# A state space layer on Trainium2: half of a product of the powers' last doubling made on ScalarE, table steps and the last group's work in another order

## The chip, the core and the metric

The kernel runs on one core of a Trainium2 chip (trn2). The metric is the device time of one execution in microseconds (us), the median of several. A core has five engines that run side by side, each with an instruction queue of its own worked through in order: TensorE (PE in the profile; its weight loads are PEld), VectorE (DVE), ScalarE (ACT), GpSimd (POOL) and SyncE (SP), which here only issues DMAs. They wait for each other through semaphores.

## The reference

The kernel computes one block over x (4096 rows of 512) with a context of 3202 rows of 384. The cross-attention layer keeps the 32 highest scores per row and head, and gives scale and shift ("film") for what goes into and out of a diagonal state space layer. Feed-forward layers follow. The change lies in the state space layer and at its two borders. Cut to that:

```python
def s4d(x, log_dt, A_re, A_im, C_re, C_im, D_skip):
    dt = jnp.exp(log_dt)
    A = A_re + 1j * A_im
    C = C_re + 1j * C_im
    dtA = dt[:, None] * A                     # 512 channels x 64 states
    dC = C * (jnp.exp(dtA) - 1.0) / A
    powers = jnp.exp(dtA[:, :, None] * jnp.arange(L))
    K = 2.0 * jnp.einsum('dn,dnl->dl', dC, powers).real
    ...                                       # y = causal convolution of x with K
    return y + x * D_skip

x = layernorm(x_text) * (1 + gate * scale_in) + gate * shift_in
y = s4d(x, ...) * (1 + gate * scale_out) + gate * shift_out
xt = x_text + y
xt = xt + gelu(layernorm(xt) @ W1 + b1) @ W2 + b2
```

## The kernel before

**Attention.** `attention` works through 128 slots (32 row tiles of 4 heads) and 8 more that drain the pipeline. A slot k does `threshold(k)` on VectorE, the logarithm of the softmax sum of head k-1 (`log_sum`, L624), its Exp (`softmax`, L648), and parts of older tiles on TensorE: `transposed` (L664), `weighted` (L685), `film` (L710), `reverse` (L752), the last of which stores the layer's input to DRAM (`x1r`, L757). A DMA on POOL adds the heads of a tile up in SBUF (L659). Engines keep the order in which the code issues (`manual_schedule`).

**Tables.** `state_space_tables` (L886) is a generator. It computes on VectorE, with a few Tanh and Sin on ScalarE, the powers of exp(dtA) that the layer needs and stores them to a DRAM scratch `tabs` (`store`, L900: powers of two on SP's queue, the rest on POOL's). `TABLE_SLOTS` (L348) says after which slots it is resumed: after 128 (loads, first exponential up to the Tanh L943), twice after 129 (angles; Tanh and Sin, L958 to L962), after 130 (six squarings) and after 134 (chunk powers and output coefficients).

**State space layer.** Channels lie in pairs: 256 pairs in 8 groups of 32. A group's work is spread over rounds g = -2 to 8 of `round_` (L1323). For a group:

- `powers(g, k)`, k = 0 or 1 (L1117): powers 0 to 63 of 16 pairs by doubling on VectorE, real and imaginary parts; five levels of two products (L1132, L1133) and a sum (L1134), into one of five power tiles of 16 KB a partition.
- `top(g, k)` (L1136): the last doubling, powers 64 to 127. ScalarE makes the product with the real factor, an activation per pair (L1140, 16 of 128x128). VectorE makes the product with the imaginary factor, two halves of 8 pairs (L1150, two of 128x1024). `top_sum` (L1153) adds them later, half by half (L1156).
- `turn` and `chunk` (L1160, L1175), u = 0 to 7: TensorE transposes four pairs' powers (L1170), ScalarE evicts them to `bt` (L1173), TensorE multiplies them with x (L1182), ScalarE evicts to the states `ht` (L1186).
- `scan_inside`, `scan_over`, `scan_into` (L1212 to L1227): recurrences over chunks on VectorE, from all of `ht`.
- `outputs` (L1229): VectorE weighs the states into `z` (L1237 to L1239), ScalarE copies z to `sz` (L1244).
- `between(g, u)`, u = 0 to 3 (L1250): TensorE products of sz and powers (L1257), in two PSUM buffers; ScalarE evicts to `yg` (L1263), POOL adds the skip term (L1265), and four DMAs on SP store rows to the scratch `kd` (L1267).
- `load_k` (L1272) reads kd back as shifted rows `hk` (two DMAs of 512 KB, four buffers), `inside` (L1283) multiplies them with x (L1291), `store` (L1296) evicts (L1298) and stores to `yT` (L1300).

In round g VectorE does scan_inside(g), top_sum(g+1, 1), scan_over(g), scan_into(g), outputs(g), powers(g+2, 0), its part of top(g+2, 0), powers(g+2, 1), top_sum(g+2, 0), and its part of top(g+2, 1). In the same round TensorE and ScalarE do turn and chunk of group g+1 with inside and store of group g-1 between them, then between(g, 0 and 1), turn and chunk 7, between(g, 2 and 3). Short-lived VectorE tiles (`tmp`, among them z and the products of top) share five buffers.

**Feed-forward.** `feed_forwards` (L1419) starts on its own weights pool, which lies where the power tiles lay. `weights(0)` (L1933) loads the first quarter of the weights on POOL's queue; `load_front(i)` (L1475) loads, for a row tile, yt from yT, x and the film rows on SP's queue. `front_a` to `front_d` (L1498 to L1528) make the layer's normalized and transposed input, and `hidden` (L1536) begins.

Of the kernel before, what the change touches and what calls it, by code (L numbers as in the profile page):

```python
# [20 lines left out]
P = 128  # L21
# [325 lines left out]
HALVES = ((0, 401), (401, 400))  # L347
TABLE_SLOTS = [NT * H + k for k in (0, 1, 1, 2, 6)]  # L348


def attention(env, io, x1r, film_out, missed, masked, tabs):
# [11 lines left out]
    with ExitStack() as ctx:  # L363
# [149 lines left out]
        setup2 = ExitStack()  # L513
        at_pool = []

        xts, xns, qT, m8s, s_of, nms, lbs, aTs, pts, pas, acTs, x1s, fs = (
# [242 lines left out]
        def slot(i, h):  # L759
# [5 lines left out]
            back = 0 <= j < NT  # L765
            log_sum(k - 1)
            if k < NT * H:
                threshold(k)
# [79 lines left out]
        for k in range((NT + 2) * H):  # L848
            if k == H:
                setup2.close()  # L850
                at_pool.append(
                    ctx.enter_context(tc.tile_pool(name="f_at", bufs=1, reuse_waits="tile"))
                )
            slot(*divmod(k, H))
            if k == NT * H:

                flat = [s_pool[0].tile([P, GP4], F32, name="s") for _ in range(2)]
                flat.append(kT.rearrange("p h g -> p (h g)"))
                steps = state_space_tables(nc, io, tabs, [
                    f[:, 3 * k * NPAIR : 3 * (k + 1) * NPAIR].rearrange("p (k q) -> p k q", k=3)  # L860
                    for f in flat for k in range(4)
                ])
            for _ in range(TABLE_SLOTS.count(k)):
                next(steps, None)
            if k < H:
                for v in range(NDV):
                    part(k, v)
# [18 lines left out]
def state_space_tables(nc, io, tabs, planes):  # L886
# [9 lines left out]
    for name in ("log_dt", "A_re", "A_im", "C_re", "C_im"):  # L896
        v[name] = new()
        nc.sync.dma_start(v[name], io[name])

    def store(k, t):  # L900
# [40 lines left out]
    k, r = exp_before(v["log_dt"])  # L941
    t = new()
    nc.scalar.activation(t, r, AF.Tanh, scale=0.5)  # L943
    yield
    dt = v["log_dt"]
# [63 lines left out]
    ts(w3[:, 2, :], w3[:, 1, :], -1.0, None, ALU.mult)  # L1009
    store(T_CHUNK + 6, w3)  # L1010

    er, den, ei = rc, kc, w[:, 1, :]
# [41 lines left out]
def state_space(env, io, tabs, x1r, yT):  # L1054
# [9 lines left out]
    with ExitStack() as ctx:  # L1064
# [71 lines left out]
        def top(g, k):  # L1136
# [8 lines left out]
            for half in range(2):  # L1145
# [3 lines left out]
                t2 = temp(NSB * n).rearrange("p (q r n) -> p q r n", q=NSB // 2, r=2)  # L1149
                mul(t2, pt[:, js, :, :n], wi.unsqueeze(3).to_broadcast(sh))  # L1150
                tops[g, k].append((js, t2))
# [98 lines left out]
        def between(g, u):  # L1250
# [61 lines left out]
        nc.gpsimd.memset(later.rearrange("p (m a) -> p m a", m=4)[:, :, 0], 0.0)  # L1312

        def zeros():
            nc.gpsimd.memset(sz[:64, :, 1, :, :], 0.0)
            nc.gpsimd.memset(sz[64:, :, 0, :, :], 0.0)
            zero = ygp.tile([P, 4, P], F32, name="yg")
            nc.gpsimd.memset(zero, 0.0)
            nc.sync.dma_start(
                kd.rearrange("(c p) l -> p c l", p=P)[:, :, : P - 1], zero[:, :, : P - 1]  # L1320
            )

        def round_(g):  # L1323
# [14 lines left out]
            if now:  # L1338
                scan_over(g)
            for u in range(4):  # L1340
                if back:
                    inside(g - 1, u)
                    if u < 2:
                        load_k(g - 1, u + 2)
                if n1 and u < 3:
# [4 lines left out]
                if u == 0 and now:  # L1350
                    scan_into(g)
            if now:
                outputs(g)
# [4 lines left out]
            if back:  # L1358
                store(g - 1, 2)
                store(g - 1, 3)  # L1360
            if n1:
                turn(g + 1, 6)
# [4 lines left out]
            for half in (0, 1):  # L1367

                if n1 and not n2 and half == 0:
                    turn(g + 1, 7)  # L1370
                    chunk(g + 1, 6)
                    chunk(g + 1, 7)
                if now:
                    between(g, 2 * half)
                    between(g, 2 * half + 1)
                    load_k(g, half)
                if n2 and n1:
                    if half == 0:
                        turn(g + 1, 7)
                    chunk(g + 1, 6 + half)  # L1380
            if n2:
                powers(g + 2, 1)
                top_sum(g + 2, 0)
                top(g + 2, 1)

        for g in range(-2, NGRP + 1):
            round_(g)
            if g == -2:
                zeros()

# [28 lines left out]
def feed_forwards(env, io, film_out, yT, x2, xq, dq, undo, out):  # L1419
# [9 lines left out]
    with ExitStack() as ctx:  # L1429
# [45 lines left out]
        def load_front(i):  # L1475
# [8 lines left out]
            else:  # L1484
# [3 lines left out]
                scale, shift = ft[:, :D], ft[:, D:]  # L1488
            fts[i] = scale, shift
            nc.sync.dma_start(yts[i], yT.rearrange("(c p) t -> p c t", p=P)[:, :, rows])  # L1490
            nc.sync.dma_start(xts[i], io["x"][rows, :])
            if i == 1:
                nc.sync.dma_start(scale, film_out[rows, :D])
                nc.sync.dma_start(shift, film_out[rows, D:])
            else:
                nc.sync.dma_start(ft, film_out[rows, :])

# [565 lines left out]
```

## Time and profile before

| | us |
|---|---|
| Median of 11 runs | 3531.47 (3525.64 to 3585.58) |
| Profiled execution | 3534.23 |
| its span | 3532.3 |
| VectorE, TensorE, ScalarE, POOL busy in the span | 3021.2, 3110.8, 2012.4, 999.3 |
| Attention's last threshold ends, VectorE | 1598.4 |
| First power of the state space layer (L1132) | 1680.03 |
| scan_inside of rounds 0 to 6 starts | 1735.42, 1790.06, 1847.77, 1904.79, 1962.10, 2019.54, 2076.81 |
| scan_inside of round 7 starts | 2123.91 |
| last inside ends | 2190.5 |
| first matmul of hidden | 2213.2 |

A profile line of the timeline gives the start and the length in us, the engine, the line of the kernel, the operation, the tiles out<-in with their shape, and how many instructions were merged into the line; in square brackets stands how long the engine stood idle before it and what ended that. In the table of stretches, a row gives the stretch, its length, the busy time of each engine with the number of instructions, the TensorE clock that was granted, the DMA engines' share and GB/s. A mean duration of a small ScalarE instruction is longer than the distance at which such instructions follow each other, since they overlap.

### The profile page before, as it was taken

Reading aid. Unit: us, or ns where it says so; the run is one execution under the profiler, and the core shown is the slowest. Engines: PE = TensorE matmul, PEld = TensorE weight load, DVE = VectorE, ACT = ScalarE, POOL = GpSimd, SP = SyncE. Lnnn points to the kernel's source line nnn. Section 1 sums busy time; section 2 is a strip of 40 time slices with the busy share of each in tenths; the row PEclk is TensorE's granted clock in tenths of the full one; section 3 lists DMA queues with packets and bytes.
Section 4 is the critical chain, followed back from the end, with each engine's and each line's share of the span. In section 5 each row is a group of like instructions: output and inputs, shape, how many; then the busy total and the mean of one; then the engine's idle time right before and its main releaser. Section 6 shows DMA issues by size and latency. Waiting matters only on the chain.

```text
span 3532.3 us, 48303 instructions
## 1 busy us (share of the span) xinstructions
PE 3110.8 (88%) x15034; PEld 1892.4 (54%) x15078; DVE 3021.2 (86%) x9391; ACT 2012.4 (57%) x3771; POOL 999.3 (28%) x1620
## 2 busy tenths in 40 slices
PE   7899999999999999996578786989999999999975
PEld 3444444444444444443567774656666666666642
DVE  5999999999999999998899983776777877777787
ACT  3777777777777777772566651223444444444445
POOL 2222222322333333332000000223334433334333
PEclk9999999999999999998678886999999999999987
DMA  7767666766666766665245446752332333332211
GB/s 199 125 136 141 133 136 134 143 137 139 132 134 138 142 134 138 128 127 140 54 117 128 113 109 186 253 103 67 59 59 58 62 59 70 69 69 57 47 40 48
DMA packets 355862, 394.19 MB, mean 112 GB/s; under 512 B 112741, under 2 KB 249959, under 8 KB 355210
## 3 DMA queue, kind: packets, MB, share of 16 engines
q0 software_dynamic: 51872, 161.82, 25.7%
q1 hardware_dynamic: 303722, 229.20, 25.7%
q8 instruction: 120, 1.97, 0.2%
q14 instruction: 148, 1.21, 0.2%
HBM read 171.31 MB, written 62.15 MB: 66 GB/s over the span
## 4 chain that ended last, share of the span: by engine, by line
PE 54%; DVE 21%; DMA 10%; ACT 7%; issue 5%; POOL 3%; SPq 0%; POOLq 0%; DVEq 0%; ACTq 0%
PE ph L1539 12%; PE po L693 12%; PE po L1550 11%; DMA s<-s 7%; DVE cand L597 3%; PE po L718 3%; PE pb L1684 3%; PE ps L580 3%; PE pp L1794 3%; ACT s L584 2%; DVE s L619 2%; PE pt L676 2%; DVE tmp L1204 1%; DVE pt L1134 1%; DVE tmp L1202 1%
## 5 line engine op out<-in xcount | busy, mean ns | idle before, releaser
L597 DVE MAX8 cand<-s 128x8 f32<-128x89 f32 (+1 forms) x4608 | 715.3, 243 | 18.7 <-ACT s L584 18.7
L693 PE MATMUL po<-ctxn,aT 124*128 124x384 f32 (+1 forms) x1664 | 634.2, 526 | 10.8 <-ACT aT L681 10.5
L1539 PE MATMUL ph<-hT,w 128*128 128x256 f32 x2048 | 503.7, 390 | 4.6 <-ACT gt L1544 4.0
L655 ACT ACTIVATE s<-s,lb 128x1601 f32<-128x1601 f32 x256 | 419.0, 1637 | 117.3 <-POOL lb L644 116.9
L1550 PE MATMUL po<-w,gt 128*128 128x512 f32 x1024 | 485.8, 597 | 0.0
L584 ACT ACTIVATE s<-ps 128x802 f32<-128x802 f32 (+1 forms) x512 | 399.9, 835 | 127.8 <-PE ps L580 127.6
L693 PEld LDWEIGHTS po<-ctxn,aT 124*128 124x128 f32 (+1 forms) x1664 | 324.1, 205 | 270.7 <-issue 70.8
L619 DVE SCALAR_TENSOR_TENSOR s<-s,m 128x3202 f32<-128x3202 f32 x128 | 455.5, 3558 | 6.9 <-DVE m L608 0.2
L1539 PEld LDWEIGHTS ph<-hT,w 128*128 128x128 f32 x2048 | 383.4, 195 | 69.7 <-issue 10.0
L1544 ACT ACTIVATE gt<-ph,b 128x256 f32<-128x256 f32 x256 | 120.9, 472 | 473.0 <-PE ph L1539 472.2
L1709 DVE SCALAR_TENSOR_TENSOR cv<-pb,cw,cv 128x256 f32<-128x256 f32 (+1 forms) x544 | 252.7, 465 | 151.7 <-ACT cv L1700 142.0
L718 PE MATMUL po<-wvf,acT 128*128 128x512 f32 x768 | 363.8, 610 | 0.6 <-ACT acT L708 0.6
L1700 ACT ACTIVATE cv<-pb,cb,cw 128x256 f32<-128x256 f32 (+1 forms) x272 | 148.8, 547 | 225.5 <-DVE pb L1693 225.2
L580 PE MATMUL ps<-kT,qT 32*128 32x401 f32 (+1 forms) x2048 | 262.7, 553 | 9.9 <-ACT s L584 9.9
L1550 PEld LDWEIGHTS po<-w,gt 128*128 128x128 f32 x1024 | 195.1, 193 | 137.6 <-issue 119.8
L659 POOL DMA_DIRECT2D s<-s x96 | 129.4, 1348 | 471.6 <-ACT s L655 152.6
L1778 POOL TENSOR_TENSOR cv<-cv,scb 128x512 f32<-128x512 f32 (+1 forms) x136 | 180.7, 1345 | 276.1 <-ACT scb L1773 276.1
L676 PE MATMUL pt<-ident,s 128*124 128x128 f32 x832 | 140.7, 301 | 104.9 <-DMA s<-s 104.9
L718 PEld LDWEIGHTS po<-wvf,acT 128*128 128x128 f32 x768 | 135.4, 189 | 180.9 <-issue 163.9
L1684 PEld LDWEIGHTS <-w1q 128*128 128x128 bf16 x1088 | 105.3, 102 | 205.4 <-issue 132.3
L1684 PE MATMUL pb<-xw,w1q 128*128 128x258 bf16 (+1 forms) x1088 | 167.7, 279 | 50.7 <-DVE cv L1709 36.2
L676 PEld LDWEIGHTS pt<-ident,s 128*124 128x124 f32 x832 | 109.8, 153 | 184.5 <-issue 153.8
(313 smaller groups left out, 5047.1 us busy)
## 6 DMA issues: line engine op xcount, KB each, us to landing
s<-s POOLq DMA_DIRECT2D x96, 1602.0 KB, 11.8
hk<-kd SPq DMA_DIRECT2D x64, 512.0 KB
film_out<-f SPq DMA_DIRECT2D x32, 512.0 KB
xt<-in_x SPq DMA_DIRECT2D x63, 256.0 KB
ft<-film_out SPq DMA_DIRECT2D x31, 512.0 KB
qT<-qd SPq DMA_DIRECT2D x128, 64.0 KB
xu<-in_x SPq DMA_DIRECT2D x32, 256.0 KB
x1r<-xr SPq DMA_DIRECT2D x32, 256.0 KB
```

Source lines behind the costliest of these rows:

```text
L580: nc.tensor.matmul(ps[:, j - j0, :n], qT[i][r, h, :], kT[r, h, c0 : c0 + n], start=True, stop=True,)
L584: nc.scalar.activation(sq[:, j0 : j0 + 2, c0 : c0 + n], ps[:, :, :n], AF.Copy, scale=QSCALE * TINY)
L597: nc.vector.max(out=cand[:, :, b], in_=s[:, b * CHW : min((b + 1) * CHW, G)])
L619: nc.vector.scalar_tensor_tensor(s[:, :G], s[:, :G], m8[:, KTOP - 1 : KTOP], s[:, :G], ALU.is_lt, ALU.subtract, accum_out=missed[:, k : k ...
L655: nc.scalar.activation(part, part, AF.Exp, bias=lbs[k][:, 1:2], scale=-1.0 / TINY)
L676: nc.tensor.transpose(pt[:w, c - 4 * g, :], s[:, c * CW : c * CW + w], ident)
L693: nc.tensor.matmul(pas[i][:, :DV], aTs[i][:w, c, :], ctxn[:w, c, :], start=(c == 0), stop=(c == NG - 1),)
L718: nc.tensor.matmul(po, acTs[i][:, c, :], wvf[:, c, q * D : (q + 1) * D], start=False, stop=(c == NDV - 1),)
L1539: nc.tensor.matmul(ph, w1[:, d, c * P : (c + 1) * P], hTs[b][:, d, :], start=(d == 0), stop=(d == ND - 1),)
L1550: nc.tensor.matmul(pos[b * TB + k], gs[b, c][:, k * P : (k + 1) * P], w2[:, c, :], start=(c == 0), stop=(c == NH - 1),)
L1684: nc.tensor.matmul(ph[:, : n + 2], w1q[:, d, c * P : (c + 1) * P], bit["xw", j][:, d, : n + 2], start=(d == 0), stop=(d == ND - 1),)
L1709: nc.vector.scalar_tensor_tensor(cv, ph[:, tap : tap + n], cw[:, c, tap : tap + 1], cv, ALU.mult, ALU.add)
```

## The change

Five parts, in the order of the code.

1. The tables' generator is made one slot before the last head, and resumed after slots 127, 129, 130, 132 and 133, and once inside slot 128 between log_sum and what follows. Its yields stand after the input loads, ahead of the first Tanh, ahead of and behind the second block of Tanh and Sin, behind the squarings, and behind the chunk powers.
2. In `top`, the second half's product with the imaginary factor is made on ScalarE, an activation for each of 8 pairs and 2 parts.
3. In the last groups: kd's stores of group 7 go on two queues by turns; the last two hk of group 7 get a home in a free power tile and are loaded in round 7; in round 6, turns and chunks 3 to 7 of group 7, scan_into and outputs come ahead of the inside products of group 5.
4. The zeros of sz are copied by ScalarE ahead of the first round, not set by POOL behind it.
5. x and film of the first two row tiles are loaded on POOL's queue.

```diff
-TABLE_SLOTS = [NT * H + k for k in (0, 1, 1, 2, 6)]
+TABLE_SLOTS = [NT * H + k for k in (-1, 1, 2, 4, 5)]
...
             log_sum(k - 1)
+            if k == NT * H:
+                next(steps[0])
             if k < NT * H:
                 threshold(k)
...
-            slot(*divmod(k, H))
-            if k == NT * H:
+            if k == NT * H - 1:
...
+                steps.append(state_space_tables(nc, io, tabs, [
...
+                next(steps[0])
+            slot(*divmod(k, H))
             for _ in range(TABLE_SLOTS.count(k)):
-                next(steps, None)
+                next(steps[0], None)
...
         nc.sync.dma_start(v[name], io[name])
+    yield
...
     t = new()
+    yield
     nc.scalar.activation(t, r, AF.Tanh, scale=0.5)
-    yield
...
     store(T_CHUNK + 6, w3)
+    yield
...
-                mul(t2, pt[:, js, :, :n], wi.unsqueeze(3).to_broadcast(sh))
+                if half:
+
+                    for j in range(js.start, js.stop):
+                        for r in range(2):
+                            nc.scalar.activation(
+                                t2[:, j - js.start, r, :], pt[:, j, r, :n], AF.Copy,
+                                scale=ptab[g][:, 3 * lv + 1 + r, k * NSB + j : k * NSB + j + 1],
+                            )
+                else:
+                    mul(t2, pt[:, js, :, :n], wi.unsqueeze(3).to_broadcast(sh))
...
-                nc.sync.dma_start(
+
+                queue = nc.gpsimd if g == NGRP - 1 and m % 2 else nc.sync
+                queue.dma_start(
...
-                hk[g, u, v] = two.tile([P, 8, P], F32, name="hk", bufs=4)
+                if g == NGRP - 1 and u >= 2:
+
+                    old = power_tiles[(2 * (g - 2) + 1) % len(power_tiles)]
+                    k = 2 * (u - 2) + v
+                    hk[g, u, v] = old.rearrange("p q r l -> p (q r) l")[:, 8 * k : 8 * k + 8, :]
+                else:
+                    hk[g, u, v] = two.tile([P, 8, P], F32, name="hk", bufs=4)
...
+        zero = ygp.tile([P, 4, P], F32, name="yg")
+        nc.gpsimd.memset(zero, 0.0)
+
         def zeros():
-            nc.gpsimd.memset(sz[:64, :, 1, :, :], 0.0)
-            nc.gpsimd.memset(sz[64:, :, 0, :, :], 0.0)
...
+            for p, m in ((0, 1), (64, 0)):
+                for r in range(2):
+                    part = sz[p : p + 64, r, m, :, :].rearrange("p a b -> p (a b)")
+                    n = NT * GP // (4 * P)
+                    nc.scalar.copy(
+                        part.rearrange("p (k b) -> p k b", k=n),
+                        z[p : p + 64].to_broadcast([64, n, 4 * P]),
+                    )
...
             if now:
                 scan_over(g)
+
+            soon = n1 and not n2
+            if soon:
+                for u in range(3, 8):
+                    turn(g + 1, u)
+                    chunk(g + 1, u - 1)
+                chunk(g + 1, 7)
+                scan_into(g)
+                outputs(g)
             for u in range(4):
                 if back:
                     inside(g - 1, u)
-                    if u < 2:
+                    if u < 2 and g < NGRP:
                         load_k(g - 1, u + 2)
...
             for half in (0, 1):
-
-                if n1 and not n2 and half == 0:
-                    turn(g + 1, 7)
-                    chunk(g + 1, 6)
-                    chunk(g + 1, 7)
                 if now:
                     between(g, 2 * half)
                     between(g, 2 * half + 1)
                     load_k(g, half)
+                    if g == NGRP - 1 and half:
+                        load_k(g, 2)
+                        load_k(g, 3)
...
+            queue = nc.gpsimd if i < 2 else nc.sync
             nc.sync.dma_start(yts[i], yT.rearrange("(c p) t -> p c t", p=P)[:, :, rows])
-            nc.sync.dma_start(xts[i], io["x"][rows, :])
+            queue.dma_start(xts[i], io["x"][rows, :])
...
-                nc.sync.dma_start(ft, film_out[rows, :])
+                queue.dma_start(ft, film_out[rows, :])
```

More of the change, by code (lines that the diff above doesn't have):

```diff
@@ L514, in attention @@
         at_pool = []
+        steps = []
         xts, xns, qT, m8s, s_of, nms, lbs, aTs, pts, pas, acTs, x1s, fs = (
@@ L853, in attention @@
                 )
-            slot(*divmod(k, H))
-            if k == NT * H:
+            if k == NT * H - 1:
                 flat = [s_pool[0].tile([P, GP4], F32, name="s") for _ in range(2)]
                 flat.append(kT.rearrange("p h g -> p (h g)"))
[L859 to L862, printed above, removed]
+                steps.append(state_space_tables(nc, io, tabs, [
+                    f[:, 3 * m * NPAIR : 3 * (m + 1) * NPAIR].rearrange("p (k q) -> p k q", k=3)
+                    for f in flat for m in range(4)
+                ]))
+                next(steps[0])
+            slot(*divmod(k, H))
             for _ in range(TABLE_SLOTS.count(k)):
-                next(steps, None)
+                next(steps[0], None)
             if k < H:
@@ L1312, in state_space @@
         nc.gpsimd.memset(later.rearrange("p (m a) -> p m a", m=4)[:, :, 0], 0.0)
+        zero = ygp.tile([P, 4, P], F32, name="yg")
+        nc.gpsimd.memset(zero, 0.0)
         def zeros():
-            nc.gpsimd.memset(sz[:64, :, 1, :, :], 0.0)
-            nc.gpsimd.memset(sz[64:, :, 0, :, :], 0.0)
[L1317 to L1321, printed above, removed]
+            z = zero.rearrange("p a b -> p (a b)").unsqueeze(1)
+            for p, m in ((0, 1), (64, 0)):
[6 more added lines that the diff above has]
+                    )
         def round_(g):
@@ L1342, in round_ @@
                     inside(g - 1, u)
-                    if u < 2:
+                    if u < 2 and g < NGRP:
                         load_k(g - 1, u + 2)
-                if n1 and u < 3:
+                if n1 and not soon and u < 3:
                     turn(g + 1, u + 3)
@@ L1349, in round_ @@
                     store(g - 1, u)
-                if u == 0 and now:
+                if u == 0 and now and not soon:
                     scan_into(g)
-            if now:
+            if now and not soon:
                 outputs(g)
@@ L1360, in round_ @@
                 store(g - 1, 3)
-            if n1:
+            if n1 and not soon:
                 turn(g + 1, 6)
@@ L1384, in round_ @@
                 top(g + 2, 1)
+        zeros()
         for g in range(-2, NGRP + 1):
@@ L1388, in state_space @@
             if g == -2:
-                zeros()
+                nc.sync.dma_start(
+                    kd.rearrange("(c p) l -> p c l", p=P)[:, :, : P - 1], zero[:, :, : P - 1]
+                )
 def quant_scales(nc, pool, mx, shape):
@@ L1489, in load_front @@
             fts[i] = scale, shift
+            queue = nc.gpsimd if i < 2 else nc.sync
             nc.sync.dma_start(yts[i], yT.rearrange("(c p) t -> p c t", p=P)[:, :, rows])
-            nc.sync.dma_start(xts[i], io["x"][rows, :])
+            queue.dma_start(xts[i], io["x"][rows, :])
             if i == 1:
-                nc.sync.dma_start(scale, film_out[rows, :D])
-                nc.sync.dma_start(shift, film_out[rows, D:])
+                queue.dma_start(scale, film_out[rows, :D])
+                queue.dma_start(shift, film_out[rows, D:])
             else:
-                nc.sync.dma_start(ft, film_out[rows, :])
+                queue.dma_start(ft, film_out[rows, :])
         def front_a(i):
```

## Prediction

> **What bounds the kernel now.** I read the page's engine line and slices first, then the chain of waits. VectorE and TensorE are both full in the attention (until about 1595 us) and in the feed-forward part (from 2213 us). The change works on what lies between, so I took the table of stretches for it, one row for each round of the state space loop (from one start of scan_inside, L1202 on 512 elements, to the next).
>
> ```profile
> PE 3110.8 (88%) x15034; PEld 1892.4 (54%) x15078; DVE 3021.2 (86%) x9391; ACT 2012.4 (57%) x3771; POOL 999.3 (28%) x1620
> ```
>
> ```profile
> core 0: us, PE busy (x) PEld busy (x) DVE busy (x) ACT busy (x) POOL busy (x), PEclk, DMA share, GB/s
> 1600.70:1680.03 79.33, 50.05 (x141) 24.31 (x139) 61.52 (x147) 19.68 (x35) 20.05 (x37) 0.84 0.50 131
> 1904.79:1962.10 57.31, 46.48 (x456) 42.06 (x456) 55.15 (x97) 34.75 (x92) 2.75 (x5) 0.82 0.50 123
> 2156.58:2190.50 33.92, 24.38 (x264) 17.53 (x264) 0.23 (x1) 5.15 (x9) 2.34 (x6) 0.71 0.78 226
> ```
>
> In a round VectorE works 55.2 of 57.3 us and ScalarE 34.8, so by shares a product moved to ScalarE looks free. The timelines of the engines in that round say otherwise.
>
> ```profile
> 1889.38 2.36 DVE L1150 TENSOR_TENSOR tmp<-pt,taba 128x1024 f32<-128x1024 f32 x2
> 1889.38 4.79 ACT L1140 ACTIVATE pt<-pt,taba 128x128 f32<-128x128 f32 x16 [3.83 <-DVE pt L1134]
> 1894.19 1.07 ACT L1263 COPY yg<-ps_y 128x512 f32<-128x512 f32 x2
> 1894.83 6.35 PE L1257 MATMUL ps_y<-pt,sz 128*64 128x128 f32 x64 [3.52 <-ACT yg L1263]
> 1903.18 0.84 ACT L1186 COPY ht<-ps_u 64x124 f32<-64x124 f32 x4 [1.33 <-PE ps_u L1182]
> 1904.05 4.78 ACT L1140 ACTIVATE pt<-pt,taba 128x128 f32<-128x128 f32 x16
> 1904.79 0.68 DVE L1202 TENSOR_TENSOR tmp<-ht,tabb 128x512 f32<-128x512 f32 x1
> ```
>
> The reader is to see a second path. When powers end (1889.38), ScalarE makes the 16 copies of top, and only then the yg evictions; TensorE stands 3.52 us waiting for the first of them, does between, then the last chunk, and ScalarE's ht copies end at 1904.05. scan_inside needs them and starts at 1904.79. VectorE's own path is only 0.74 us longer here; over the six rounds the slack is 1.33, 1.20, 0.74, 0.48, 1.66, 1.30 (mean 1.1).
>
> **The steady change, priced.** Each of 16 calls of top loses one L1150 on VectorE (2.36 us for two that overlap; 1.14 us each as spaced) and gets 16 activations of 128x64 on ScalarE, 256 in all. None of that shape is in the trace. L1140 (128x128, same operands) comes every 0.299 us (4.79 / 16); sz copies L1244 take 1.05 us for 1024, so an element costs (1.05 - 0.299) / 896 = 0.84 ns, and 64 fewer make 0.245. Bounds: 0.21 (L1186, 0.84 us for four of 64x124) and 0.299. I take 0.245: A = 3.93 us per call (3.4 to 4.8).
>
> The Trainium skill ("ScalarE: Activation LUTs", What ACT_TABLE_LOAD costs) gives 186 ns plus 0.833 ns per element, 93 more per pointer operand, 93 of overlap, which makes an estimate of 0.239 us here and takes 1.4 us from the sum below. The same page (Rules for kernel authors) says that a multiplication belongs on VectorE and not on ScalarE. By the rows it is 3.93 us there against 1.14 on VectorE.
>
> *Rounds 0 to 5, the path from powers to ht.* The products stand in ScalarE's queue between L1140 and yg, so yg, between, the last chunk and ht all come A later. ht was ready 14.13, 14.20, 14.70, 14.93, 13.74 and 14.10 us after the powers ended; with 3.93 each that is 109.4 us, against 92.5 (6 x 15.42) on VectorE's path, which shrinks to 13.1 and no longer decides. **+16.9 us** (13.6 to 22). What is saved on VectorE returns as waiting for ht, 5 us a round.
>
> *The z buffers.* The other call of top (end of the round) delays the bt evictions: products end 8.7 us after scan_inside starts, L1140 alone ended 3.2 to 4.8 after it. TensorE's turn, chunk and inside run without a gap from there, so the ht copies ahead of the sz copies come 3.9 to 5.6 later, and so does the sz copy. VectorE's powers reuse the buffer that sz reads:
>
> ```profile
> 1934.19 2.58 ACT L1244 COPY sz<-tmp 64x1024 f32<-64x1024 f32 x2
> ...
> 1938.80 0.29 DVE L1132 TENSOR_TENSOR tmp<-pt,taba 128x128 f32<-128x128 f32 x1
> ```
>
> The semaphore instructions of L1132 stand ahead of its second and fifth levels in rounds with outputs, and not in the round without; I read them as this reuse. Today the copy is done 2.0 us ahead. Then it would end at about 1940.9, 2.1 late; worked through, rounds 0 to 5 give 0.3, 4.5, 2.3, 2.1, 2.5 and 4.6. The large ones rest on slow matmuls in two rounds; I take 2.0 a round, **+12** (0 to 16).
>
> *The start (rounds -2 and -1).* top_sum(0,1) waits for ScalarE's products at 27 us after the powers start instead of ending at 26.2; bt starts 2.7 late; the next top adds 3.93 before the last bt and ht. **+6.6** (5.5 to 8.4).
>
> **The tables, moved ahead.**
>
> ```profile
> 1608.14 0.29 DVE L919 TENSOR_SCALAR kT<-kT 128x256 f32<-128x256 f32 x1 [7.47 <-ACT kT L943]
> 1669.83 0.42 DVE L1036 TENSOR_TENSOR s<-kT 128x256 f32<-128x256 f32 x1 [2.92 <-DMA tabs<-s]
> 1680.03 0.23 DVE L1132 TENSOR_TENSOR tmp<-pt,taba 128x64 f32<-128x64 f32 x1 [3.08 <-DMA tabs<-s]
> ...
> 1668.66 0.37 SPq L1105 DMA_DIRECT2D taba<-tabs  x1
> ```
>
> The Tanh L943 had its input at 1600.66 but stood behind softmax and film copies until 1607.69. Now it stands behind log_sum (done 1595.94): VectorE goes on at 1601.2, 6.9 earlier. It holds ac, acT, two Exp and the film copies for 3 to 4 us; nothing is lost, since the accumulating DMA of that softmax waits until 1610.6 for the one before, and TensorE's next transposes for its landing (1623.34). Whether the Exp after it need a second table load no row shows: 0 to 1.28 us (L943's load), inside the same cover. The skill's page (Table sets) puts exp and tanh in one set, so none by it. The 2.92 wait goes too, because the chunk powers are stored from POOL three slots sooner, ahead of input_film. POOL loses two memsets of sz (1.80 each, one ahead of the last table store); their four ScalarE copies (4 x 1.05) lie in its idle 14.38 us ahead of 1688.55, and would cost up to 4.2 without it.
>
> The tables end at about 1665.3 instead of 1675.16. What is late next is the taba load, on SP behind the last x1r store, 7.2 us to land. That chain began with an aT copy at 1628.26, held by Tanh and Sin on ScalarE although its transposes were there at 1624.1; they now come first, 4.1 us saved. taba lands at 1671.8 and the powers start at 1672.2: **-7.8** (-3 if half the chain holds, -9.9 if VectorE alone decides).
>
> **The end of the layer.**
>
> ```profile
> 2123.91 0.69 DVE L1202 TENSOR_TENSOR tmp<-ht,tabb 128x512 f32<-128x512 f32 x1 [14.01 <-ACT ht L1186]
> 2156.58 10.78 PE L1257 MATMUL ps_y<-pt,sz 128*64 128x128 f32 x128 [2.63 <-ACT sz L1244]
> 2180.34 1.21 PE L1291 MATMUL ps_h<-hk,xg 128*32 128x128 f32 x16 [4.72 <-DMA hk<-kd]
> 2196.86 0.55 DVE L78 TENSOR_SCALAR r<-xt,stats 128x512 f32<-128x512 f32 x1 [33.20 <-DMA xt<-in_x]
> ```
>
> Counted from scan_inside of round 6 (2076.81): with turns and chunks of group 7 together (2.67 us each, as in round -1) ht is ready at +35, not +47, and VectorE's last sz input at +66, not +78. But TensorE has inside(6) ahead of between(7), and that hangs on kd and hk of group 6, whose start moves only 1.7 us: between(7) starts at +75.5 instead of +79.8 (-4.3). After it, 16 kd stores at 0.6 us on one queue become eight on SP and eight on POOL (0.75 each), and all hk loads go out at once; POOL's stores must land first (about 2.5 us), and eight hk loads are 4 MB, 10 us at the 400 GB/s seen later. The last inside ends 26.5 us after between starts instead of 33.9 (-7.4). On the other side, hk's new home is power tile 1; ident_bf waiting for between (L1944, 9.04 us) tells that the weights lie over the power tiles, so the first weights wait for the last inside, and x and film behind them on POOL; the film landed 9.9 us after it before, and 1 MB of weights takes 7.3 to 9.2. I take -0.3. Together **-12** (-5 to -27, the latter if film and x are there before yt, and inside(6) holds nothing).
>
> **Sum.** -7.8 + 6.6 + 16.9 + 12 - 12 = +15.7. The profiled execution took 3534.23 (span 3532.3 and 1.9 around it), 2.8 over the median of 3531.47: 3549.9 on its own terms, 3547.2 against the median.
>
> **Rivals.**
> 1. *No stall on the z buffers* (another buffer is free there): +3.7, 3535. For it: VectorE waits nowhere there now. Against: the semaphores. Chance 0.20.
> 2. *The end gives little and the stall is full*, inside(6) and the weights holding the last round: 16.3 for 12 and -3 for -12, tables -3: +34 at most, +26 likely, 3557. 0.20.
> 3. *Faster: the products don't stand ahead of yg.* If yg is late by no more than the 1.1 us of slack, rounds shorten by that slack (6 x 1.1 = 6.6), the start by two L1150 (2.3), no stall: -7.8 - 2.3 - 6.6 - 12 = -28.7, 3503. It decides below 1.1 us per call, 0.07 us an activation; in the sum, at 14 us per us of A, the sign turns at A = 2.8 (0.175 each). For it: ScalarE is idle 22 us a round. Against: the shortest spacing seen is 0.21, and the queue keeps its order. With the end at its best included, 0.15.
> 4. The forecast: 0.45.
>
> **Numbers.** A measurement of this kernel tells about 0.2% (7 us) from no change. Slower: 0.45 + 0.20 and a part of rival 1, 0.69; within: 0.18; faster: 0.13. The range 3520 to 3566 takes in rivals 1 and 2 and the ends of the unknown costs, leaving out most of rival 3.
>
> **What would show it.** L1150 16 times; 256 activations near 0.33 us long, 0.245 apart; rounds of 60 to 63 us, with some 5 us a round of L1202 waiting for ht and about 2 of L1132 waiting for sz; the first powers near 1672; the 14.01 wait gone; hidden's start 10 to 14 us sooner counted from round 6. Wrong if rounds stay at 57 or below, or if the end gains over 25.

## The result and the profile after

The kernel after takes 3568.72 us (median of 10 runs) against 3534.88 of the kernel before (37 runs); the ratio is 1.0102 [1.0092, 1.0112], about +36 us. A second set of runs (after2 below) gave 1.0097 [1.0082, 1.0112]. The forecast was +15.7, and its range ended at 3566. Some executions of most kernels here have an attention 80 to 100 us longer than the rest: the ratios leave them out, the profiles of e3, e4, e8 and e10 to e13 are of this kind and are read for the state space layer and its borders alone, and e13 has no ratio because all its runs were.

The engine line of the page of after, and its table of stretches for the same three stages as before (tables, one round, last group):

```profile
PE 3111.6 (87%) x15034; PEld 1889.0 (53%) x15078; DVE 2996.1 (84%) x9375; ACT 2079.6 (58%) x4031; POOL 975.6 (27%) x1631
```

```profile
core 0: us, PE busy (x) PEld busy (x) DVE busy (x) ACT busy (x) POOL busy (x), PEclk, DMA share, GB/s
1612.91:1689.59 76.68, 56.46 (x167) 27.95 (x165) 60.37 (x152) 27.87 (x49) 18.02 (x40) 0.91 0.61 153
1939.76:2004.65 64.89, 47.05 (x456) 41.82 (x456) 52.25 (x93) 42.30 (x125) 2.19 (x5) 0.76 0.45 109
2215.71:2241.20 25.49, 22.01 (x268) 15.20 (x264) 0.28 (x1) 4.70 (x8) 4.95 (x12) 0.80 0.73 200
```

VectorE has 16 instructions less and 25 us less work, ScalarE 260 instructions and 67 us more. The round is 64.89 us long instead of 57.31, although VectorE works 2.9 us less in it: it was full but for 2.2 us, and now it stands idle 12.6, of which 10.6 are two waits. The timelines of that round say for what:

```profile
1939.75 4.78 ACT L1146 ACTIVATE pt<-pt,taba 128x128 f32<-128x128 f32 x16
1944.44 3.92 ACT L1160 ACTIVATE tmp<-pt,taba 128x64 f32<-128x64 f32 x16
1948.38 1.08 ACT L1188 COPY bt<-ps_t 128x512 f32<-128x512 f32 x2
1949.02 1.97 PE L1185 MATMUL ps_t<-ident,pt 128*128 128x128 f32 x8 [9.30 <-ACT bt L1188]
1950.78 3.51 PE L1197 MATMUL ps_u<-xg,bt 128*128 128x64 f32 x16
...
1976.36 4.45 ACT L1259 COPY sz<-tmp 64x1024 f32<-64x1024 f32 x4
1978.72 0.29 DVE L1138 TENSOR_TENSOR tmp<-pt,taba 128x128 f32<-128x128 f32 x1 [5.76 <-ACT sz L1259]
...
1986.61 4.78 ACT L1146 ACTIVATE pt<-pt,taba 128x128 f32<-128x128 f32 x16 [3.00 <-DVE pt L1140]
1991.30 3.91 ACT L1160 ACTIVATE tmp<-pt,taba 128x64 f32<-128x64 f32 x16
1995.24 1.08 ACT L1278 COPY yg<-ps_y 128x512 f32<-128x512 f32 x2
1995.87 5.90 PE L1272 MATMUL ps_y<-pt,sz 128*64 128x128 f32 x64 [7.86 <-ACT yg L1278]
2003.78 0.84 ACT L1201 COPY ht<-ps_u 64x124 f32<-64x124 f32 x4 [1.33 <-PE ps_u L1197]
2004.65 0.69 DVE L1217 TENSOR_TENSOR tmp<-ht,tabb 128x512 f32<-128x512 f32 x1 [4.83 <-ACT ht L1201]
```

The reader is to see the 16 new activations (L1160) in two seats, that is, two places in ScalarE's queue. The **first seat**, when a round starts, stands ahead of the bt copies: TensorE waits 9.30 us (5.47 before, in the lines of the section on the prediction), and its next transposes and chunk products take 1.97 and 3.51 us where they take 1.05 and 1.96 later in the round. The sz copies come late and VectorE's powers wait 5.76 us. The **second seat** stands ahead of yg: TensorE waits 7.86 us (3.52 before), ht is late, scan_inside waits 4.83.

This first profiled execution (3586.44) was 18 us above the median: its last threshold ended 13 us later than in after2, the second profile of the same kernel, and its tables took 7 us longer. The stages below are therefore taken from after2. "Orders alone" is the kernel after without the new activations (e1 and e15 below). What lies behind hidden's start is left out: with the same instructions, it took 1306 to 1319 us in the profiles of this study, 1309 and 1318 in the two of the orders alone. It took 11 us less in after2 than in before, so their spans are only 22.4 us apart where the stages add up to +32.2 and the ratio says +34.

| stage, us | before | after2 | orders alone (e15) | predicted change | measured change |
|---|---|---|---|---|---|
| last threshold to first power (L1132, L1138) | 81.6 | 69.8 | 70.8 | -7.8 | -11.8 |
| first power to scan_inside(0) | 55.4 | 62.4 | 55.8 | +6.6 | +7.0 |
| rounds 0 to 5 | 341.4 | 381.4 | 341.8 | +28.9 | +40.0 |
| scan_inside(6) to last inside | 113.7 | 105.8 | 100.3 | -11.7 | -7.9 |
| last inside to hidden | 22.7 | 27.6 | 27.6 | -0.3 | +4.9 |
| sum | | | | +15.7 | +32.2 |

### The profile page after: what moved, and what is told of

It reads as the page before. It is cut to its first block, busy times and chain, and to the rows that moved or that the text cites. A ratio compares the mean times of both kernels' runs of the same rounds, so it can differ in the third digit from the quotient of the medians.

```text
span 3584.5 us, 48562 instructions
## 1 busy us (share of the span) xinstructions
PE 3111.6 (87%) x15034; PEld 1889.0 (53%) x15078; DVE 2996.1 (84%) x9375; ACT 2079.6 (58%) x4031; POOL 975.6 (27%) x1631
## 3 DMA queue, kind: packets, MB, share of 16 engines
q8 instruction: 120, 1.97, 0.2%
## 4 chain that ended last, share of the span: by engine, by line
PE 49%; DVE 20%; issue 15%; DMA 6%; ACT 6%; POOL 3%; SPq 0%; POOLq 0%; DVEq 0%; ACTq 0%
PE ph L1579 12%; PE po L1590 11%; PE po L694 10%; DVE cand L598 8%; DVE s L620 5%; DMA s<-s 3%; PE po L719 3%; PE pb L1724 3%; PE pp L1834 3%; PE ps L581 2%; ACT s L585 2%; DVE m L609 2%; DVE w L614 1%; PE pt L677 1%; DMA xq<-xbT 1%
## 5 line engine op out<-in xcount | busy, mean ns | idle before, releaser
L656 ACT ACTIVATE s<-s,lb 128x1601 f32<-128x1601 f32 x256 | 419.1, 1638 | 105.9 <-POOL lb L645 105.8
## 6 DMA issues: line engine op xcount, KB each, us to landing
s<-s POOLq DMA_DIRECT2D x96, 1602.0 KB, 11.8
```

Of the source, the lines that this page charges most:

```text
L656: nc.scalar.activation(part, part, AF.Exp, bias=lbs[k][:, 1:2], scale=-1.0 / TINY)
```

## The experiments

All ratios are to the kernel before, on the same chip. The waits are those of VectorE, in the rounds that have them; in rounds 0 and 1 they are often shorter.

| kernel | ratio | rounds 0 to 5, us | wait for sz, a round | wait for ht, a round | scan_inside(6) to hidden |
|---|---|---|---|---|---|
| before | 1 | 341.4 | none | none | 136.4 |
| after2 | 1.0097 [1.0082, 1.0112] | 381.4 | 5.6 | 4.7 | 133.4 |
| e1 orders | 0.9943 [0.9928, 0.9958] | 341.0 | none | none | 127.2 |
| e2 product | 1.0137 [1.0119, 1.0154] | 381.0 | 5.6 | 4.7 | 142.3 |
| e3 sz early | 1.0049 [1.0036, 1.0063] | 363.3 | 0 to 1.6 | 2.4 to 4.4 | 133.9 |
| e6 first seat | 1.0035 [1.0012, 1.0059] | 360.3 | 0 to 1.7 | 4.4 to 5.7 | 128.4 |
| e4 second seat | 1.0033 [1.0019, 1.0047] | 359.4 | 4.6 | 2.4 | 134.9 |
| e7 all | 0.9972 [0.9960, 0.9984] | 348.1 | none | none | 126.6 |
| e8 warm, 7 | 1.0097 [1.0082, 1.0112] | 380.4 | 5.7 | 4.8 | 132.2 |
| e11 warm, 11 | 1.0021 [1.0010, 1.0032] | 358.9 | none | 4.4 to 5.7 | 127.9 |
| e9 all 2 | 0.9970 [0.9956, 0.9983] | 343.3 | none | 1.7 to 3.0 | 130.0 |
| e10 sp | 0.9955 [0.9937, 0.9972] | 341.5 | none | none | 126.3 |
| e12, e14 yg first | 0.9931 [0.9917, 0.9945], 0.9930 [0.9911, 0.9948] | 330.2, 330.5 | 0 to 1.9 | 0.2 | 127.3, 129.0 |
| e15 orders 2 | 0.9948 [0.9930, 0.9967] | 341.8 | none | none | 127.8 |

**Orders or product?** e1_orders: the ScalarE branch in `top` is replaced by the VectorE product.

```diff
-                if half:
-                    for j in range(js.start, js.stop):
...
-                else:
-                    mul(t2, pt[:, js, :, :n], wi.unsqueeze(3).to_broadcast(sh))
+                mul(t2, pt[:, js, :, :n], wi.unsqueeze(3).to_broadcast(sh))
```

> The change without its second part: VectorE makes both half products again, all the orders stay as in the kernel after. Theory (the loss is the ScalarE product's alone): by the stages of the two traces the orders gained about 5 us ahead of the powers, about 2 from the sixth round to the hidden layer and about 3 behind it, so this kernel takes 3525 +- 4, some 10 us under the kernel before, and its rounds 0 to 5 last 57 us each as before. The prediction's own terms for the orders (-7.8 and -12) would give 3515. Rival (part of the loss comes from the orders: the stores of kd on two queues, the early block of group 7, the zeros on ScalarE): 3535 to 3550.

e2_product: that branch alone, put into the kernel before.

> The kernel before with the ScalarE product alone, none of the orders. Theory (product and orders simply add): 3535 plus 9 at the start and 39 in rounds 0 to 5, so about 3580; each round near 65 us, with a wait of VectorE near 5.5 us for the copies of sz and near 5 us for ht. The prediction's terms (6.6 + 28.9) would give 3570. Rival (the product costs only together with the new orders): 3535 to 3555, rounds near 57 us.

after2: the kernel after, unchanged.

> The kernel after, unchanged, for a second profile of it beside its own variants. Theory: its first profiled execution (3586) was 18 us above its median only because the attention's last slots and the tables ran late in it, so here the table stage (last threshold to the first copy of the powers) takes about 69 us, as in the kernel with the orders alone (67.0) and not 76.4, while rounds 0 to 5 take 380 us in all and the sixth round to the hidden layer 134 us again; 3569. Rival: the tables gain nothing where the product is there too: 76 us again.

Measured: the orders gain 20 us, where the prediction's terms -7.8 and -12 gave 19.8; the theory from the first, late profile had said 10. That the sum fits so well is luck: in e15 the tables gave -10.8 and the end -8.6. The product costs 48 us without the orders; with them, from e1 to after2, 54. Orders and product add, within the intervals. In after2 the table stage is short too, so the late tables of the first profile were that execution's own.

**The wait for sz.** e3_sz_early issues the sz copies two steps sooner on ScalarE.

```diff
-            if now and not soon:
-                outputs(g)
+                if u == 1 and now and not soon:
+                    outputs(g)
```

> The kernel after with the outputs (and so ScalarE's four copies to sz) issued behind the second of the four steps of turn, chunk and inside, not behind the fourth; VectorE's order is the same. Theory (the wait of the powers' second level for the sz copies is on the ring, but ScalarE itself is the next limit, since it idled only 3.0 us ahead of the high-half copies): the wait falls from 5.6 to about 2 us, rounds 1 to 5 get about 3 us shorter each, 3553 in all. Rival 1 (the wait is on the ring in full, as the sum of the prediction took it): up to 3.9 us a round, 3548. Rival 2 (the wait has slack behind it, the ring is set by the products ahead of yg alone): 3568, unchanged, the 3 us reappear as a longer wait for ht.

Measured: the wait falls from 5.6 us to 0 to 1.6, rounds 1 to 5 from 64.9 to 59.8 to 61.7, the ratio by 0.0048 (17 us): the wait is on the path that sets the round. Rounds 1 to 5 lose 3.9 us each, as rival 1 said; round 0 is 1.2 us longer.

**The first seat.** e6_place1 splits `top`, and issues the ScalarE product of k = 1 behind turns 0 and 1.

```diff
-                top_sum(g + 1, 1)
                 turn(g + 1, 0)
                 turn(g + 1, 1)
+                products(g + 1, 1)
...
             if now:
                 scan_over(g)
+            if n1:
+                top_sum(g + 1, 1)
```

> The kernel after with the ScalarE product of the second half of each group (the one that runs when a round starts) issued behind the transposed copies bt of turns 0 and 1, not ahead of them, and its sum on VectorE behind the scan over blocks. Theory (TensorE's long wait for bt, 9.3 us, is what makes its next 13.6 us of matmuls slow and so makes sz late): the wait for bt falls to about 5.4 us as before the change, the slow stretch ends some 4 to 6 us sooner, the wait for sz falls from 5.6 to 0 to 2 us, rounds get 3 us shorter (ScalarE is next), 3550. Rival (the slow stretch has nothing to do with the wait, and only 3.9 us of order are won): sz copies 3.9 us sooner, nearly the same gain of time, but the transposes L1185 of turns 1 and 2 still near 1.95 us and the products of chunks 0 and 1 near 3.5. Rival 2 (no slack anywhere on VectorE): 3568.

Measured: -0.0062 against after2, 21 us in rounds 0 to 5 and 5 us behind them. TensorE's wait is 5.47 us again, but what follows it differs from round to round. Round 3, and round 4:

```profile
1915.91 1.97 PE L1185 MATMUL ps_t<-ident,pt 128*128 128x128 f32 x8 [5.47 <-ACT bt L1188]
1917.67 3.51 PE L1197 MATMUL ps_u<-xg,bt 128*128 128x64 f32 x16
...
1977.19 1.97 PE L1185 MATMUL ps_t<-ident,pt 128*128 128x128 f32 x8 [5.47 <-ACT bt L1188]
1978.95 3.51 PE L1197 MATMUL ps_u<-xg,bt 128*128 128x64 f32 x16
1982.27 1.88 PE L1185 MATMUL ps_t<-ident,pt 128*128 128x128 f32 x8
1983.96 2.00 PE L1197 MATMUL ps_u<-xg,bt 128*128 128x64 f32 x16
1985.78 1.04 PE L1308 MATMUL ps_h<-yg,later 128*128 128x512 f32 x2
```

In rounds 2 and 3 the matmuls behind the wait are slow for 13.6 and 13.8 us, counted to the first group at its usual time, as long as in after2 behind 9.30 us of waiting (the rival's case), and VectorE waits 1.6 and 1.7 us for sz. In rounds 1, 4 and 5 they are slow for 7 to 9 us, and VectorE does not wait for sz (the theory's case). So part of the gain is the order and part a shorter slow stretch, and the length of the wait alone does not set that stretch. Whether waiting sets the stretch at all is the next question. e8_warm and e11_warm11 put products on TensorE that nothing reads between turns 0 and 1 of each round (seven and eleven):

```diff
                 turn(g + 1, 0)
+                if now:
+                    idle = ps_h.tile([P, 4 * P], F32, name="ps_h")
+                    for _ in range(11):
+                        nc.tensor.matmul(
+                            idle, later, xg[g].rearrange("p a c -> p (a c)")[:, : 4 * P],
+                            start=True, stop=True,
+                        )
                 turn(g + 1, 1)
```

> The kernel after with seven products of 128x512 more on TensorE in each round, between the transposes of turns 0 and 1, whose result nothing reads; they fill 7.3 of the 9.3 us in which TensorE waits for bt. Theory (the slow matmuls follow the wait): the transposes of turn 1 and the products of chunks 0 and 1 take 1.05 and 1.96 us, not 1.97 and 3.51, so the sz copies come about 4 us sooner, the wait for sz falls from 5.6 to about 1.5, rounds get 3 us shorter, 3553. Rival (the slow stretch comes of something else, such as the whole round's load): the matmuls stay slow, rounds 65 us or, where the added products run slow themselves, longer, 3570 to 3600.

> As e8_warm, but with eleven products, which fill TensorE's whole wait for bt (seven took 6.2 us and left 3.3 us, and the granted clock was still 0.51 for the next 13.6 us). Theory (any idle stretch of some 3 us brings the low clock, and none is left here): granted clock near 1.0 and transposes of 1.05 us behind them, sz copies 4 to 5 us sooner, wait for sz near 1 us, rounds 62 us, 1.005 of the kernel before. Rival (the low clock follows from the stage, idle or not): transposes near 1.97, chunk products near 3.5, rounds 65 us or more, 1.010.

Seven changed nothing. They took 6.17 us and left a wait of 3.28, and the matmuls behind it were as slow as ever. Timeline and stretches of e8_warm (the stretches: the added products, the wait, what follows):

```profile
2021.37 6.17 PE L1363 MATMUL ps_h<-xg,later 128*128 128x512 f32 x14
2030.82 1.97 PE L1185 MATMUL ps_t<-ident,pt 128*128 128x128 f32 x8 [3.28 <-ACT bt L1188]
2032.58 3.52 PE L1197 MATMUL ps_u<-xg,bt 128*128 128x64 f32 x16
```

```profile
2021.40:2027.50 6.10, 6.10 (x16) 2.44 (x14) 5.73 (x9) 6.08 (x23) 0.00 (x0) 1.00 0.56 162
2027.60:2030.80 3.20, 0.00 (x0) 0.00 (x0) 3.13 (x6) 3.17 (x13) 0.00 (x0) 0.92 0.68 181
2030.80:2044.40 13.60, 13.58 (x82) 12.01 (x82) 12.81 (x36) 4.46 (x13) 0.00 (x0) 0.52 0.17 27
```

Eleven left no wait. Timeline and stretch of e11_warm11:

```profile
1996.94 9.61 PE L1363 MATMUL ps_h<-xg,later 128*128 128x512 f32 x22
2006.39 1.15 PE L1185 MATMUL ps_t<-ident,pt 128*128 128x128 f32 x8
2007.38 1.95 PE L1197 MATMUL ps_u<-xg,bt 128*128 128x64 f32 x16
```

```profile
2007.20:2020.80 13.60, 13.60 (x154) 11.84 (x152) 12.81 (x36) 7.97 (x21) 0.00 (x0) 1.00 0.47 115
```

The reader is to compare the PEclk column: 0.52 against 1.00 over the same 13.6 us, where nearly twice as many matmuls pass (154 against 82). The wait for sz is gone, rounds 0 to 5 are 22.5 us shorter, and the ratio falls by 0.0076 (27 us) although TensorE does more work than in after. In e8 the added products ran at 1.00 and the clock fell at the end of the 3.2 us left empty behind them, so it is the empty stretch that brings it down: the theory on the clock is shown. The forecast of 62 us a round was 2 too long.

**The second seat.** e4_place0 issues the product of k = 0 behind the first two yg evictions, and the sum that reads it behind scan_inside of the next round.

```diff
                     between(g, 2 * half + 1)
                     load_k(g, half)
...
+                if n2 and half == 0:
+                    products(g + 2, 0)
...
-                top_sum(g + 2, 0)
+                top_sum(g + 2, 0, slice(0, 1))
```

> The kernel after with the ScalarE product of the first half of each group issued behind the first two evictions yg instead of ahead of them, into ScalarE's idle time there, and the sum that needs it on VectorE moved behind the inner scan of the next round. Theory (the 3.9 us ahead of yg delay yg, the next product of TensorE, the last chunk and ht in full): ht and so the next round come 3.9 us sooner, VectorE's wait for ht falls from 4.8 to about 1 us, the wait for sz stays near 5.5 us, rounds 0 to 5 take 61 us each, 3545 in all. Rival (the ring closes over the other product and the sz copies, and gives it back there): rounds near 64, 3565. The unmoved product at the start of the round and the wait for sz are the same in both.

Measured: rounds 2 to 5 near 61.4 us, 1.0033, 23 us under after2: the theory's numbers. The wait for ht is 2.4, not 1.

**Both seats.** e7_all joins e3, e4 and e6.

> The kernel after with all three moves: both ScalarE products behind the copies they delayed, and the sz copies behind the second step. Nothing is left out. Theory (the loss is only where the products stand, not that ScalarE makes them): VectorE becomes the bound again with its two half products (2.46 us a round) gone, rounds 1 to 5 take 55 to 56 us against 57.4 of the kernel with the orders alone, and the kernel takes 3500 to 3510, below both kernels and below the orders alone (3515 on the scale of the kernel before at 3535). Rival (ScalarE's added 7.8 us a round are too much in any place): rounds of 58 to 60, 3520 to 3535, above the orders alone.

The rival's number: 58.3 us a round, 0.9972. The waits for sz and ht are gone and two others took their place:

```profile
1942.00 1.60 PE L1185 MATMUL ps_t<-ident,pt 128*128 128x128 f32 x8 [4.51 <-ACT bt L1188]
1946.84 5.31 PE L1272 MATMUL ps_y<-pt,sz 128*64 128x128 f32 x64
1952.19 0.20 DVE L1127 COPY pt<-taba 128x32 f32<-128x32 f32 x1 [3.00 <-PE ps_y L1272]
```

The sz copies, issued two steps sooner, wait for VectorE in ScalarE's queue; the bt copies behind them come late, between runs late and slow, and VectorE's next powers wait for the power tile that between still reads. e9_all2 issues the outputs one step later (`u == 2`).

> All three moves as in e7_all, but the outputs (and the sz copies) are issued behind the third step, not the second. In e7_all VectorE no longer waited for sz or ht, but 3.0 us a round ahead of the second half's powers for TensorE's product out of the power tile, and TensorE had idled 4.5 us for bt behind sz copies that themselves waited for VectorE, and ran at half clock after it. Theory (with the copies one step later TensorE goes on, the wait for the power tile goes, VectorE with two half products less is the bound): rounds 1 to 5 take 55 to 56 us, the kernel is 0.989 to 0.992 of the kernel before and beats the one with the orders alone (0.9943). Rival (the products' 7.8 us on ScalarE show up in another wait): rounds near 58 as in e7_all, 0.997.

The rival again, 0.9970: the wait for the power tile went, and ht was 1.7 to 3.0 us late, since yg still stood behind the 4.8 us of high-half copies (the product with the real factor, L1146):

```profile
1943.01 4.79 ACT L1146 ACTIVATE pt<-pt,taba 128x128 f32<-128x128 f32 x16 [3.82 <-DVE pt L1140]
1947.82 1.08 ACT L1278 COPY yg<-ps_y 128x512 f32<-128x512 f32 x2
1948.46 6.67 PE L1272 MATMUL ps_y<-pt,sz 128*64 128x128 f32 x64 [3.45 <-ACT yg L1278]
```

e12_yg_first puts these copies behind yg as well, and the product behind turn 7 and chunk 6; e13_yg_chunk_first puts both behind turn 7 and chunk 6.

```diff
                 powers(g + 2, 0)
-                top(g + 2, 0)
...
                 if n2 and half == 0:
-                    products(g + 2, 0)
+                    top(g + 2, 0)
                 if n2 and n1:
...
+                if n2 and half == 0:
+                    products(g + 2, 0)
```

> As e9_all2, with ScalarE's high-half copies of the first half behind the first two evictions yg as well, and the ScalarE product behind the copies of turn 7 and chunk 6. In e9_all2 VectorE still waited 2.9 us a round for ht: yg stood behind the 4.8 us of high-half copies, and TensorE idled 3.5 us for it. Theory (with both seats freed VectorE is the bound and saves its two half products, 2.4 us a round): no wait for ht, rounds 1 to 5 of 55 to 56 us, 0.990 to 0.992, below the orders alone (0.9943). Rival (ScalarE's 7.8 us more a round move into another wait): rounds of 57 to 58, 0.995 to 0.998.

> As e12_yg_first, with turn 7 and chunk 6 ahead of the high-half copies too, and the copies and the product directly behind each other. Theory: as e12_yg_first, rounds of 55 to 56, 0.990 to 0.992; the high-half copies start some 2 us later, which VectorE's first sum has to spare. Rival (that sum waits for them): rounds 2 us longer than in e12_yg_first.

e12 fell to rounds of 55.5 us, as the theory had it, but to 0.9931, a little above the 0.990 to 0.992 it gave. e13's rounds 1 to 5 took 56 to 57 us, 0.5 to 0.9 over those of e12, where the rival had 2. e12 and the orders alone were then run side by side:

> The kernel of e12_yg_first again, beside the kernel with the orders alone on one chip. Theory (rounds of 55.5 us against 57.3, and the first scan 3 to 6 us sooner): 13 to 17 us under the orders alone. Rival (the stages of its first profile, whose attention ran disturbed, overstate it, as its ratio of 0.993 says): 0 to 6 us under it, and a stage outside the rounds is longer by the difference.

> The kernel with the orders alone again, as the other side of that comparison: 0.9943 of the kernel before, rounds 0 to 5 in 341 us, the first copy of the powers 67 us behind the last threshold, 127 us from the sixth round to the hidden layer.

Spans 3504.4 against 3513.3 us, -8.9, between the theory's 13 to 17 and the rival's 0 to 6: -11.3 in rounds 0 to 5, +2.2 from the last threshold to scan_inside(0), +1.2 from scan_inside(6) to hidden and -1.2 behind it. The ratios, 0.9930 [0.9911, 0.9948] and 0.9948 [0.9930, 0.9967], overlap: both versions beat both kernels of this study, but whether e14 also beats the orders alone is clear in the profiles' rounds only. In its round ScalarE works 42.00 us, as in after (42.30), and VectorE waits 0.2 us for ht; the last between runs beside the high-half copies and starts without a wait (7.86 in after):

```profile
1892.70:1948.20 55.50, 44.57 (x458) 39.94 (x457) 53.20 (x93) 42.00 (x124) 2.78 (x5) 0.84 0.51 127
```

```profile
1935.95 4.80 ACT L1146 ACTIVATE pt<-pt,taba 128x128 f32<-128x128 f32 x16 [0.47 <-DVE pt L1140]
1937.57 4.37 PE L1272 MATMUL ps_y<-pt,sz 128*64 128x128 f32 x64
1942.46 3.93 ACT L1162 ACTIVATE tmp<-pt,taba 128x64 f32<-128x64 f32 x16
```

**The end.** e10_sp is e1_orders with x and film of the first row tiles back on SyncE's queue (`queue = nc.sync`).

> The kernel with the orders alone (VectorE makes both half products), and x and film of the first two row blocks back on SyncE's queue behind the load of yT, instead of on GpSimd's. Theory (from the last product of inside to the hidden layer all kernels with the orders take 27.6 us against 22.7 before, since yT, x, film and 2 MB of weights move together): that stage falls by 2 to 3 us, 0.9935 of the kernel before. Rival (the weights alone hold yT back): 27.6 us again or longer, 0.9943 to 0.995.

The stage from the last inside to hidden took 25.7 us, not 27.6; the total (0.9955 [0.9937, 0.9972]) can't be told from that of e1. So x and film beside the load of yT make some 2 of the 4.9 us. The other 3 were not isolated, but the traces show where they lie. The last store of yT is issued 0.7 us behind the last inside in every one of these kernels. SyncE then waits for its landing before it loads yT: that load is issued at +3.0 us in the kernel before and at +6.5 to +6.9 in after2, e15 and e10. The first weights start at +0.3 and +1.1 us there, and at -21.8 and -21.0 before. That they hold up the store is the likely cause; no run moved them.

## Why the prediction was wrong

The sign, the two seats and both waits were right; three terms were mis-sized: against the forecast the z buffers came out 10.5 us dearer, the end 9.0 dearer and the tables 4.0 cheaper, and the other two terms 1.0 dearer together.

- **The z buffers: 2.0 us a round was forecast, 5.6 came.** This is the step that failed most. The working gave 4.5 and 4.6 to rounds 1 and 5 and called these large ones the slow matmuls' doing "in two rounds". In the kernel before, the slow stretch lasted 13.8 and 13.6 us in those rounds and 6.8 to 9.0 in rounds 2 to 4; in after2 it lasts 13.5 or 13.6 in each of rounds 1 to 5. Round 3 of before, then of after2:

```profile
1909.49 1.97 PE L1170 MATMUL ps_t<-ident,pt 128*128 128x128 f32 x8 [5.47 <-ACT bt L1173]
1916.27 2.23 PE L1182 MATMUL ps_u<-xg,bt 128*128 128x64 f32 x16
1918.32 1.05 PE L1285 MATMUL ps_h<-yg,later 128*128 128x512 f32 x2
...
1927.67 1.97 PE L1185 MATMUL ps_t<-ident,pt 128*128 128x128 f32 x8 [9.30 <-ACT bt L1188]
1937.76 2.01 PE L1308 MATMUL ps_h<-yg,later 128*128 128x512 f32 x2
1939.70 1.64 PE L1314 MATMUL ps_h<-hk,xg 128*32 128x128 f32 x32
1941.27 1.10 PE L1185 MATMUL ps_t<-ident,pt 128*128 128x128 f32 x8
```

The forecast carried the slow matmuls over as they lay, instead of asking what makes them slow, and then took less than its own six rounds add up to (16.3). e11 shows it: without TensorE's wait the sz term is zero, and rounds 0 to 5 shrink by 22.5 us against the 12 of the sum. So does round 1 of the first profile of after, the only one of its rounds 1 to 5 with a short slow stretch (8.9 us): the wait for sz is 3.2 us in it and 5.4 to 5.8 in rounds 2 to 5.
- **The second seat: +16.9 forecast.** What e11 leaves over the kernel before is 358.9 - 341.4 = 17.5, with 4.4 to 5.7 us a round of waiting for ht where 5 was said. Right. A was 3.92 us as forecast at 3.93.
- **The start: +6.6 forecast, +7.0 measured.** The product alone (e2) gives +6.9, and the orders alone +0.4 in e15 but +2.9 in e1. Right.
- **The tables: -7.8 forecast, -11.8 measured**, beyond the -9.9 of its range. Tanh behind log_sum came as said. The step that failed is the taba load, which was to be late behind the x1r chain and to take 7.2 us: the last x1r store is issued 6.4 us sooner, not 4.1, and the first copy out of taba (L1127) starts without a wait 3.6 us after the load is issued (1662.29). VectorE's last wait is for a table store:

```profile
1601.77 0.29 DVE L924 TENSOR_SCALAR kT<-kT 128x256 f32<-128x256 f32 x1 [0.48 <-ACT kT L949]
...
1665.89 0.20 DVE L1127 COPY pt<-taba 128x32 f32<-128x32 f32 x1
1669.28 0.22 DVE L1138 TENSOR_TENSOR tmp<-pt,taba 128x64 f32<-128x64 f32 x1 [3.18 <-DMA tabs<-s]
```

- **The end: -12 forecast, -3.0 measured.** Two parts failed. The stage from the last inside to hidden was put at -0.3 and is +4.9: 27.5 to 27.9 us in every kernel with the orders but e10 (25.7), against 22.7. The working followed x, film and the weights; the load of yT behind its late store was not in it. And the product's own cost there was left out: the first seat stands at the start of round 6 too, so that round lasts 36.9 us up to scan_inside(7) in after2 and 32.1 in e15; e6 (33.1) and e11 (30.9) get it back. The orders alone give -13.4 up to the last inside, against -11.7 forecast.
- **The rivals.** Rival 2 (the end gives little, the stall is full; 3557, +34 at most) has the two terms that failed on the right side. That its upper end is the measured size is luck: it has 16.3 for the stall, where 22.5 came, and -3 for the tables, where -11.8 came. It had 0.20. Rival 1 (no stall) falls with the 28.1 us of waits for sz in after2. Rival 3 (products not ahead of yg) is what e12 and e14 make by hand, with other copies moved as well: rounds 0 to 5 are then 11.3 us shorter than with the orders alone.

Not settled: what decides how long the slow stretch lasts. Behind the same wait of 5.47 us it has 6.8 to 9.0 us in some rounds of the kernel before and 13.6 or more in others, and behind 9.29 us it had 8.9 in round 1 of the first profile of after. The traces' clock records hold one hint. Any two changes of the clock in a trace are a whole number of steps of 3.41 us apart. A round of 64.9 us is 19 such steps (64.85), so each round meets the steps at the same places; a round of 57.3 us is 16.8 of them. That fits the equal stretches of after2, and no run varied it.

## What to carry to other kernels

Work moved to an engine with idle time costs what stands behind it in that engine's queue: here 3.9 us of ScalarE time twice a round cost 22 to 27 us a seat. Moving the same instructions behind the evictions, and the sz copies forward, brought 33 of the 40 us back (e7); rounds shorter than with the orders alone came only when the high-half copies moved too (e14). When a wait of TensorE grows, or is met in a new place, price the matmuls behind it at half clock too, and treat slow matmuls in a trace as an effect with a cause, not as a fixed place. Carry each price of a repeated stage into the last repetitions as well, where it meets the other parts of a change.

## What the runs showed of the hardware

TensorE's granted clock has two values in these traces, 1.00 and 0.50; a share like 0.52 is a mean over a stretch. It fell to 0.50 with waits of 3.28, 5.47 and 9.30 us at the start of a round, and after the wait it stayed there for long, by the clock records: 13.0 to 13.4 us in four of e8's five rounds behind 3.28, 3.5 to 13.5 us in e1_orders behind 5.47, 12.9 to 13.1 in rounds 1 to 5 of after2 behind 9.30. With the wait filled with work (e11), it stayed at 1.00. Behind the waits of 7.8 us for yg it came back sooner, after 3.5 to 3.8 us of products of between. One of these in the profile of after:

```profile
1995.87:1999.71 3.84, 3.84 (x36) 3.84 (x38) 3.84 (x4) 2.16 (x8) 1.71 (x2) 0.50 0.03 6
1999.71:2003.00 3.29, 3.29 (x43) 3.17 (x40) 0.12 (x1) 1.15 (x2) 0.48 (x3) 1.00 0.09 16
```

The Trainium skill ("TensorE: Matmul & The Clock Gate", What's actually happening) says that an idle window of about 3.4 us halves the clock and that about 3.4 us of sustained work restores it. The first half agrees with these waits, the shortest of them 3.28 us; but a step of 3.41 us at 0.50 also came 0.7 us behind a wait of 2.17 us in round 3 of the kernel before. The second agrees with the stretches behind the waits for yg and with the shortest one at the start of a round (3.5 us in e1_orders); most of those are two to four times the page's figure.
